# A sixteen-stage kernel: query blocks of the causal attention in another order, zero products ahead of units, and the last block of latent keys projected later

## The chip, the core and the metric

The kernel runs on one core of a Trainium2 chip. The core has a matrix engine (TensorE, PE in the profile; its weight loads are shown as PEld), a vector engine (VectorE, DVE), an engine for activations (ScalarE, ACT), GpSimd (POOL) and SyncE (SP), whose queue issues the transfers. TensorE reads SBUF and writes PSUM. The metric is the time of one execution on the device in microseconds.

## The reference

The reference is a chain of sixteen residual layers on `x` of 2048 tokens by 128 features: `x = x + f(layernorm(x))`, for four blocks of two mixers and two feed-forward layers each. Two of the mixers matter here.

- `L0_attn_b` is causal attention with 16 heads of width 8, with a rotary embedding of queries and keys: `q`, `k` and `v` are projected with biases, `q` and `k` are turned by cosines and sines of the position, scores above the diagonal are masked, softmax over the keys, product with `v`, projection `Wp`. In the kernel this is the stage `Causal`.
- `L1_attn_b` is latent attention with 8 heads: queries and keys come from 32 latent features each plus 32 rotary-like features (`W_QR`, `W_KR`), the scores are taken over all 2048 keys with the scale 1/sqrt(160), softmax, product with values from the latent ones, projection `W_O`. In the kernel this is the stage `Mla`.

## The kernel before

The tokens stand in four blocks of 512 (`NB`, `BW`), 128 tokens to a tile. The stages run one after another: CumSum, Moe0, Causal, Moe0, Mamba, Mla, Ssm, Moe2, Attn2, Moe2, Hale, Moe3, Filtered, Moe3. `Core.run` (line 69) interleaves them in program order: while the `main` of one stage runs, `feed` (line 114) opens the next stage and runs its `early(b)` for the blocks whose `x` is final, as `Stage.blocks` (line 227) lets it: a block starts when the `final` of the stage before exceeds its number. All stages before Hale are handed to a scheduler that orders each engine's instructions by its own time line, so the order on an engine is not that of the program text. Within the attention stages, the products that pass through `in_turn` (line 657) keep their program order on TensorE.

**Causal** (`Attn16`, lines 685 to 949). `early(b)` normalizes a block (`normed`, `turned`), projects values, makes the rotated key heads (`heads`, line 732: eight products into two banks, cosine and sine tables loaded from memory, two VectorE products, one POOL add, a split into two rounded parts) and copies them into key slots `at_KT` (`slot`, line 754), four groups `g` of four heads with a row offset for each head. Blocks 0 to 2 are done beside the stage before. Block 3 (`own = 1`) is done beside the first units, by the generator `left`, one step for each step of pass A. `heads("q", 0)` is called at the start of `main`.

The work is cut into units `(g, b)`, 16 in all, in the order of `units` (line 604): for each query block `b` from 0 to 3 its four groups. Each unit is done twice. Pass A (line 807) computes the scores query by key and takes the largest on VectorE (`at_mx`, line 833; on diagonal tiles after adding a mask, line 832). The negative maximum is transposed and written by transfers (`at_mT`, `at_q`, lines 852 and 854) into two spare rows of the unit's queries. Pass B (line 861) computes the scores key by query (line 900), masks the diagonal tile by a product (line 903), takes the exponential on ScalarE (line 906), and multiplies with the values into the accumulator `ps_c` (line 879). Four products of a 128x32 zero tile `zerob` with a tile of ones follow each of these (line 883). Unit (g, b) has b+1 chunks of 512 keys in either pass. Pass A runs ahead of pass B by one unit and some steps. After the last group of a block, `out` (line 935) adds the projected result to `x` (line 948) and sets `final`.

**Mla** (`Mla`, line 1307 on). `early(b)` normalizes, makes queries `ml_QT`, latent features `ml_Z` and values, and then for each of the 8 heads a key block: a product with `G` (line 1406) and `combine` (line 1371), that is a ScalarE copy, a second product that adds the rounding error (line 1376) and a ScalarE copy into `ml_KT` (line 1377). All four blocks are complete before `main`. `main` closes the pools down to `sm`, allots its own and runs 17 units (the first one in two halves): pass A (line 1443, reduction line 1444), the maximum by `ml_mT` into `ml_pad` (lines 1464 and 1466), pass B (lines 1496, 1498, 1483).

## Time and profile before

| quantity | value |
|---|---|
| median of three runs | 4843.47 us |
| the runs | 4835.28, 4843.47, 4845.85 us |
| profiled execution | 4842.59 us |
| its span, first to last instruction | 4840.6 us |
| mean granted TensorE clock | 0.922 |
| Causal, first pass A product to last add to `x` | 318.2 to 860.9 us |
| Mla, products of pass B | 1320.3 to about 1927 us |

The page gives busy time of each engine, the span in 40 slices of 121 us with a digit for each (tenths busy; for `PEclk`, tenths of full TensorE clock), and the chain of work that ended last. A table by stretch gives start:end and length, then the busy time and number of instructions of each engine, the mean granted clock of TensorE, the share in which the transfer engines were busy and GB/s. A line of the timeline gives start, duration, engine, line, operation, output and inputs, shapes, count, and in brackets the idle time before it with what ended it.

### The profile page before, as it was taken

The numbers are of one execution on the slowest core, as the hardware profiler recorded it, in microseconds if no ns is written. First come the engines' busy times: TensorE is split into PE (matmuls) and PEld (weight loads), VectorE is DVE, ScalarE is ACT, GpSimd is POOL, SyncE is SP. The second block draws the span as 40 slices with busy tenths as digits, with TensorE's granted clock in tenths as the row PEclk, the third lists the DMA queues.
The fourth block names the chain that finished last, engine by engine and source line by source line (L and its number), as shares of the span: only waits on it lengthen the run. The fifth ranks groups of instructions, "written<-read, shape, count | busy, mean of one in ns | idle before, by whom it ended". The sixth has DMA issues, their size and how long they took to land.

```text
span 4840.6 us, 89173 instructions
## 1 busy us (share of the span) xinstructions
PE 4411.5 (91%) x36388; PEld 2496.4 (52%) x36388; DVE 3713.6 (77%) x5694; ACT 3052.4 (63%) x5570; POOL 947.6 (20%) x826
## 2 busy tenths in 40 slices
PE   6979999988799998799999999989988989999998
PEld 4744444655344443463444457656656634444466
DVE  7867886689666653789999958457768879999777
ACT  4634667775355555356888875345546648888876
POOL 4730000544100000330000013012215600000056
PEclk9966899998699999888999999889998969999999
DMA  1010000000000000000000000112211000000000
GB/s 52 6 45 6 4 2 9 22 1 17 17 14 14 18 14 4 8 1 2 2 2 2 2 4 12 33 50 51 51 48 37 9 8 2 2 2 2 2 20 7
DMA packets 69484, 73.33 MB, mean 15 GB/s; under 512 B 17616, under 2 KB 44102, under 8 KB 69076
## 3 DMA queue, kind: packets, MB, share of 16 engines
q1 hardware_dynamic: 69076, 67.64, 5.0%
q8 instruction: 287, 4.70, 0.4%
q14 instruction: 121, 0.99, 0.1%
HBM read 32.09 MB, written 1.05 MB: 7 GB/s over the span
## 4 chain that ended last, share of the span: by engine, by line
PE 68%; DVE 21%; ACT 5%; issue 3%; POOL 2%; DMA 1%; SPq 0%; POOLq 0%; ACTq 0%; DVEq 0%
PE ps_c L879 15%; PE ps_a L829 10%; PE ps_c L1483 5%; DVE at_mx L833 4%; PE ps_b L900 4%; PE ps_a L1443 3%; PE ps_c L883 3%; PE ps_b L1496 3%; PE ps_b L148 2%; PE ps_a L148 2%; PE ps_a L150 2%; PE ps_b L149 2%; PE ps_a L149 2%; PE ps_b L150 2%; DVE m_hl L455 1%
## 5 line engine op out<-in xcount | busy, mean ns | idle before, releaser
L906 ACT ACTIVATE at_P<-ps_b 128x512 f32<-128x512 f32 (+2 forms) x2688 | 1414.4, 581 | 335.0 <-PE ps_b L900 211.1
L833 DVE TENSOR_REDUCE at_mx<-ps_a 128x2 f32<-128x1024 f32 (+2 forms) x1344 | 1537.7, 1184 | 106.5 <-PE ps_b L900 66.8
L879 PE MATMUL ps_c<-at_P,at_V 128*32 128x256 f32 (+3 forms) x10752 | 868.3, 396 | 7.8 <-ACT at_u L888 7.3
L900 PE MATMUL ps_b<-at_q,at_KT 32*128 32x512 f32 (+2 forms) x2688 | 759.5, 499 | 6.6 <-DMA at_q<-at_mT 5.0
L829 PE MATMUL ps_a<-at_KT,at_q 32*128 32x512 f32 (+3 forms) x2688 | 701.1, 521 | 48.0 <-DVE at_mx L833 45.7
L829 PEld LDWEIGHTS ps_a<-at_KT,at_q 32*128 32x128 f32 x2688 | 267.1, 196 | 497.4 <-issue 338.1
L1444 DVE TENSOR_REDUCE ml_mx<-ps_a 128x2 f32<-128x1024 f32 x256 | 305.4, 1222 | 216.4 <-PE ps_a L1443 215.4
L454 ACT ACTIVATE m_hh<-ps_a,moe_b 128x512 fp32r<-128x512 f32 x512 | 349.8, 689 | 189.1 <-DVE m_h L451 158.0
L455 POOL TENSOR_TENSOR m_hl<-m_h,m_hh 128x512 fp32r<-128x512 f32 x256 | 360.5, 1409 | 541.1 <-ACT m_hh L454 529.3
L1498 ACT ACTIVATE ml_P<-ps_b 128x512 f32<-128x512 f32 (+1 forms) x544 | 272.5, 576 | 231.8 <-PE ps_b L1496 229.7
L879 PEld LDWEIGHTS ps_c<-at_P,at_V 128*32 128x32 f32 x10752 | 215.8, 110 | 359.2 <-issue 181.0
L883 PE MATMUL ps_c<-wide,zerob 128*32 128x256 bf16 x5184 | 391.1, 282 | 0.0
L266 POOL TENSOR_TENSOR ln_rs<-ln_ve,nhalf 128x4 f32<-128x4 f32 x56 | 61.8, 1104 | 1650.3 <-DVE ln_ve L264 1641.4
L900 PEld LDWEIGHTS ps_b<-at_q,at_KT 32*128 32x128 f32 x2688 | 326.3, 189 | 73.5 <-issue 44.2
L455 DVE TENSOR_TENSOR m_hl<-m_h,m_hh 128x512 fp32r<-128x512 f32 x256 | 257.1, 1005 | 79.4 <-ACT m_hh L454 77.9
L453 ACT ACTIVATE m_h<-ps_a,moe_b 128x512 f32<-128x512 f32 x320 | 220.6, 690 | 77.1 <-DVE m_hl L455 42.0
L1483 PE MATMUL ps_c<-ml_P,ml_V 128*33 128x512 f32 (+3 forms) x1088 | 257.5, 596 | 2.9 <-ACT ml_P L1498 2.9
L148 PE MATMUL ps_b<-m_hh,moe_w2h 128*128 128x512 f32 x512 | 221.7, 433 | 20.7 <-DVE m_t L475 17.8
L149 PE MATMUL ps_b<-m_hl,moe_w2h 128*128 128x512 f32 x512 | 213.9, 418 | 26.4 <-DVE m_hl L455 20.7
L148 PE MATMUL ps_a<-ln_h,moe_w1h 128*128 128x512 f32 x512 | 218.7, 428 | 10.7 <-ACT m_hh L454 10.6
L883 PEld LDWEIGHTS <-zerob 128*32 128x32 bf16 x5184 | 156.1, 100 | 113.6 <-issue 10.8
L149 PE MATMUL ps_a<-ln_l,moe_w1h 128*128 128x512 f32 x512 | 207.4, 405 | 0.0
(655 smaller groups left out, 7759.7 us busy)
## 6 DMA issues: line engine op xcount, KB each, us to landing
hl_KS<-hl_pkh SPq DMA_DIRECT2D x160, 64.0 KB
moe_w_raw<-in_l0f_W SPq DMA_DIRECT2D x32, 256.0 KB
ml_pad<-ml_QT SPq DMA_DIRECT2D x32, 256.0 KB
moe_w_raw<-in_l3f_W SPq DMA_DIRECT2D x32, 256.0 KB
hl_KS<-hl_pkl SPq DMA_DIRECT2D x80, 64.0 KB
at_pad<-at_q SPq DMA_DIRECT2D x64, 64.0 KB
at_q<-at_mT SPq DMA_DIRECT2D x192, 4.0 KB
at_cosT<-in_cosT SPq DMA_DIRECT2D x8, 256.0 KB
```

Source lines behind the costliest of these rows:

```text
L148: nc.tensor.matmul(out, lh, rh, start=start, stop=False)
L149: nc.tensor.matmul(out, lh, rl, start=False, stop=False)
L454: nc.scalar.activation(hh, ph, AF.Relu, bias=bias)
L455: (nc.gpsimd if f in ((0, 2) if self.spare else MS) else nc.vector).tensor_tensor(hl, h, hh.bitcast(F32), ALU.subtract)
L829: self.in_turn(nc.tensor.matmul(pa[:, k, :w], q[r, i * P : (i + 1) * P], KT[r, ch * BW : ch * BW + w], start=True, stop=True))
L833: nc.vector.tensor_reduce(mx[:, i, 2 * jj : 2 * jj + 2, ch], pa[:, :, :w], AX.X, ALU.max)
L879: self.in_turn(nc.tensor.matmul(self.acc[32 * j : 32 * j + 32, s], self.V[:, kt, h : h + 32], ps[j][:, s], start=start, stop=stop))
L883: self.in_turn(nc.tensor.matmul(self.acc[32 * j : 32 * j + 32, z], c.zerob, c.wide[:, z], start=False, stop=False))
L900: self.in_turn(nc.tensor.matmul(pbs[k][:, off:end], KT[r, kt * P : (kt + 1) * P], q[r, off:end], start=True, stop=not diag))
L906: nc.scalar.activation(p[:, off:end], pbs[k][:, off:end], AF.Exp, scale=scale)
L1444: nc.vector.tensor_reduce(mx[:, i, :, ch], pa, AX.X, ALU.max)
L1483: self.in_turn(nc.tensor.matmul(self.acc[64 * j : 64 * j + m, s], v, ps[k][j][:, s], start=kt + k == 0, stop=kt + k == NT - 1))
```

## The change

In Causal:

- The query blocks are taken in the order 0, 2, 3, 1 (`order`). `final` rises only over blocks that are all through (`over`).
- `heads("q", 0)` moves from `main` to the end of `early(0)`.
- Cosine and sine tables have two buffers each, and the split heads of keys and queries share two tiles with two buffers each (`twice`).
- Ahead of pass B of each unit of blocks 0 and 1 (`warmed`) stand six products of a 128x128 zero tile with 512 columns of ones. For the first unit they write a bank of their own, later they add zero to the accumulator.

In Mla:

- For block 3, `early` stops after the values; the eight key heads become the generator `left`. Pass A draws from it until the heads that it needs are there (`heads`), and one more at each step (`tick`).
- Ten zero products stand ahead of the transposes of block 3's normalized tokens.
- The pool `ml_e`, which the key heads use, now outlives the start of `main`; `ml_mT`, `ml_u` and `ml_Y` have one buffer in place of two.

```diff
-        self.zerob = self.per.tile([P, 32], BF16, name="zerob")
+        self.zerob = self.per.tile([P, P], BF16, name="zerob")
...
+    def zeros(self, n, to=None):
+        first = to is None
+        to = self.ps("c") if first else to
+        return [self.nc.tensor.matmul(to, self.zerob, self.wide, start=first, stop=first) for _ in range(n)]
...
-        units = [(g, b, 0, 4) for b in range(NB) for g in range(4)]
+        units = [(g, b, 0, 4) for b in self.order for g in range(4)]
...
+    def over(self, b):
+        self.through.add(b)
+        while self.final in self.through:
+            self.final += 1
...
         for _ in self.project(b, ln):
             yield
+        if b == self.order[0]:
+            self.qhl = self.heads("q", b)
+            yield
...
-            cos, sin = [c.load(self.pre_k, "at_" + n, (P, BW), c.ins[n][:, s], bufs=1) for n in ("cosT", "sinT")]
+            cos, sin = [c.load(self.pre_k, "at_" + n, (P, BW), c.ins[n][:, s], bufs=self.twice) for n in ("cosT", "sinT")]
...
-        h, l = (self.pre_k.tile([P, BW], F32R, name=f"at_{which}{k}", bufs=1) for k in "hl")
+        h, l = (self.pre_k.tile([P, BW], F32R, name=f"at_{which if self.twice == 1 else ''}{k}", bufs=self.twice) for k in "hl")
...
-        self.qhl = self.heads("q", 0)
         self.prep(0, 0)
...
-        if g == 3 and b + 1 < NB:
-            self.need(b + 2)
-            self.qhl = self.heads("q", b + 1)
+        if g == 3 and b != self.order[-1]:
+            b1 = self.order[self.order.index(b) + 1]
+            self.need(b1 + 1)
+            self.qhl = self.heads("q", b1)
...
         q, KT = self.qb[(g, b)], self.KT[g]
+        if b in self.warmed:
+            for i in c.zeros(6, self.acc):
+                self.in_turn(i)
...
-        self.final = b + 1
+        self.over(b)
...
 class Causal(Attn16):
...
+    order = (0, 2, 3, 1)
+    warmed, twice = (0, 1), 2
...
+    def tick(self):
+        if self.heads[-1]:
+            next(self.left, None)
...
         xn = self.normed(b)
         yield
+        if b == NB - 1:
+            c.zeros(10)
         ln = self.turned(xn)
...
+        if b < NB - 1:
+            yield from self.keys(b, Z)
+        else:
+            self.left = self.keys(b, Z)
+
+    def keys(self, b, Z):
+        c, nc = self.c, self.c.nc
         for h in range(8):
             pk = c.ps("b")
             nc.tensor.matmul(pk, self.G[:, h, :], Z, start=True, stop=True)
-            self.combine(self.KT[h][:, s], pk, self.lomask)
+            self.combine(self.KT[h][:, b * BW : (b + 1) * BW], pk, self.lomask)
+            self.heads[b] = h + 1
             yield
...
         for n, (i, ch) in enumerate(steps):
-            self.need(ch + 1)
+            while self.heads[ch] < 2 * g + 2:
+                next(self.left)
...
-            mT = self.wk.tile([4, BW], F32R, name="ml_mT")
+            mT = self.wk.tile([4, BW], F32R, name="ml_mT", bufs=1)
...
-                self.u = self.wk.tile([P, BW], F32, name="ml_u")
+                self.u = self.wk.tile([P, BW], F32, name="ml_u", bufs=1)
...
-            self.Y[b] = self.wk.tile([P, 4, 8, 32], F32, name="ml_Y")
+            self.Y[b] = self.wk.tile([P, 4, 8, 32], F32, name="ml_Y", bufs=1)
```

More of the change, by code (lines that the diff above doesn't have):

```diff
@@ L568 @@
     pace = 12
+    order = tuple(range(NB))
     lead = 0.15
@@ L576, in start @@
     def start(self):
-        self.have, self.count = NB - self.own, 0
+        self.have, self.count, self.through = NB - self.own, 0, set()
         self.left = self.blocks(self.have, NB)
@@ L677, in finish_late @@
         while self.closed != u:
-            if u == (3, NB - 1, 0, 4):
+            if u == (3, self.order[-1], 0, 4):
                 self.later(2)
@@ L690 @@
     finish = Attention.finish_late
-    causal, rope = False, False
+    causal, rope, twice = False, False, 1
+    warmed = ()
     scale = 1.0 / math.sqrt(8.0)
@@ L708, in open_kv @@
         self.V, self.Vh = paired_values(self.c.nc, wp, NT, "at_V")
-        self.Y, self.qb, self.hl, self.late, self.due, self.closed = {}, {}, {}, [], [], None
+        self.Y, self.qb, self.hl, self.late, self.due, self.closed, self.acc = {}, {}, {}, [], [], None, None
     def weights(self, wp):
@@ L882, in av @@
                 if not (kt == nkt - 1 and half):
-                    self.in_turn(nc.tensor.matmul(self.acc[32 * j : 32 * j + 32, z], c.zerob, c.wide[:, z], start=False, stop=False))
+                    self.in_turn(nc.tensor.matmul(self.acc[32 * j : 32 * j + 32, z], c.zerob[:, 0:32], c.wide[:, z], start=False, stop=False))
             if kt == nkt - 1 and half:
@@ L1366, in open_kv @@
         nc.gpsimd.memset(self.V0, 0.0)
+        self.pre_k = self.pool("ml_e", 2)
         self.open_ln()
-        self.pre_k = self.pool("ml_e", 2)
         self.npad, self.qb, self.Y, self.late, self.due, self.closed = 0, {}, {}, [], [], None
+        self.heads = [0] * NB
+    def tick(self):
+        if self.heads[-1]:
+            next(self.left, None)
     def combine(self, dst, src, mask):
@@ L1415, in main @@
         self.wk = self.pool("ml_k", 2)
-        self.start()
+        self.have, self.through = NB, set()
         self.prep(0, 0)
@@ L1533, in out @@
         nc.vector.tensor_tensor(xb, po, xb, ALU.add)
-        self.final = b + 1
+        self.over(b)
 class Ssm(Stage):
```

## The prediction

> **What bounds the kernel now.** I read the page first (shares, then the slices with the granted clock, then the chain), then tables of busy time over stretches that I cut at the units of the two stages the change touches, then the timeline of VectorE and TensorE where a stretch looked wrong.

> ```profile
> span 4840.6 us, 89173 instructions
> PE 4411.5 (91%) x36388; PEld 2496.4 (52%) x36388; DVE 3713.6 (77%) x5694; ACT 3052.4 (63%) x5570; POOL 947.6 (20%) x826
> ...
> PEclk9966899998699999888999999889998969999999
> ...
> PE 68%; DVE 21%; ACT 5%; issue 3%; POOL 2%; DMA 1%; SPq 0%; POOLq 0%; ACTq 0%; DVEq 0%
> ```

> TensorE carries 68% of the chain, but its clock falls to 0.6 in slices 3 and 4 (242 to 484 us, where Causal starts) and in slice 11 (1210 to 1331 us, where Mla starts). The table by stretch (busy us and count of PE, PEld, DVE, ACT, POOL; then the clock) says what that is worth:

> ```profile
> 284.00:318.00 34.00, 21.90 (x58) 12.36 (x58) 13.00 (x22) 11.06 (x18) 5.92 (x5) 0.54 0.26 79
> 318.00:388.00 70.00, 62.12 (x406) 29.12 (x409) 48.62 (x93) 23.75 (x54) 2.53 (x2) 0.50 0.05 17
> 388.00:504.00 116.00, 109.63 (x1040) 51.20 (x1032) 87.05 (x153) 58.07 (x129) 3.57 (x3) 0.70 0.02 6
> 504.00:639.00 135.00, 127.94 (x1528) 59.08 (x1528) 121.67 (x166) 90.85 (x190) 3.39 (x13) 0.92 0.02 4
> 639.00:813.00 174.00, 169.47 (x2025) 76.02 (x2025) 152.02 (x186) 123.27 (x250) 1.02 (x1) 0.90 0.01 2
> 813.00:861.00 48.00, 45.63 (x577) 21.74 (x565) 1.66 (x5) 38.15 (x80) 0.81 (x1) 1.00 0.06 19
> ...
> 1276.00:1287.00 11.00, 6.48 (x20) 4.15 (x20) 6.71 (x24) 2.14 (x7) 3.54 (x3) 0.69 0.10 39
> 1287.00:1306.00 19.00, 18.23 (x26) 7.99 (x26) 0.29 (x1) 8.99 (x17) 0.00 (x0) 0.50 0.16 62
> 1306.00:1321.00 15.00, 11.95 (x26) 5.31 (x24) 13.20 (x14) 1.04 (x3) 0.00 (x0) 0.61 0.00 0
> ```

> The first six rows are Causal: head, pass A of query blocks 0, 1, 2, 3, and the last pass B. A chunk is 512 keys of one unit; blocks 0 to 3 hold 4, 8, 12, 16 chunks. At clock 0.92 block 2 takes 135/12 = 11.2 us a chunk with VectorE at 90%; block 1 at 0.70 takes 116/8 = 14.5 with VectorE at 75%; block 0 at 0.50 takes 17.5. So a warm TensorE leaves VectorE as the bound, a slow one binds itself. The last three rows are the start of Mla: 19 us in which TensorE projects keys at half clock and VectorE does nothing. VectorE's timeline names it: its next reduction waits 19.69 us for the scores.

> ```profile
> 1284.94 2.35 DVE L1444 TENSOR_REDUCE ml_mx<-ps_a 128x2 f32<-128x1024 f32 x2
> 1306.98 5.75 DVE L1444 TENSOR_REDUCE ml_mx<-ps_a 128x2 f32<-128x1024 f32 x5 [19.69 <-PE ps_a L1443]
> ```

> **Part 1, first query heads in `early`, two buffers for cos, sin and heads.** Before, after the last key slot of block 2, TensorE starts the query heads at 306.17 and the first pass A product runs at 318.24. In the changed order of instructions these 8 products stand behind block 1's key heads, and the query slots follow block 2's key slots at once. The moved chain is 306.17 to 313.68 (8 products, 2 VectorE products, 1 POOL add, 1 ACT cast, 1 VectorE subtraction). Its place is idle: TensorE sits 6.29 us before 289.67. Its two loads (cos, sin) move on SP's queue ahead of the Moe weight loads; those have until 861. Gain 8 us. Bounds: 12.07 (318.24-306.17) if all goes, 3.7 if block 2's heads, which share the single `at_r0`, are pushed by one rotation (L747 at 298.21 to `at_kl`'s end at 303.98, 5.8 us; 9.5-5.8). I take -8, near the first, since 290.4 to 298.2 is free on that chain.

> **Part 2, six zero products before each unit of blocks 0 and 1.** 48 products of 128x512. Nearest rows: products of 512 columns follow each other every 0.43 us at clock 0.5 (306.89 to 307.49 and on) and every 0.23 us at 1.0 (860.27, 860.50, 860.73). Block 0: 24 x 0.43 = 10.3 us, on the path, because TensorE is busy 62 of 70 us there. Against it: if the runs lift the clock, block 0 is bounded by VectorE's 48.6 us, a gain of at most 70-48.6 = 21. Ends +10.3 and -21. The clock did rise for single windows at denser moments in 388 to 504, and the runs are back to back over all 128 columns, so I take a net -5. Block 1: 24 x 0.23 = 5.5 us, hidden under VectorE if warm (I put 0), 10.3 if cold. The runs carry no wait of their own; behind each stand the next score products, and VectorE's reductions wait for those.

> [...]

> **Part 3, order 0, 2, 3, 1.** Counting each slot as the larger of pass A of a unit and pass B of the one before, both orders need 44 chunks: the long last pass B (4 chunks) becomes 2 for block 1's last unit, and 2 are lost where block 3's last pass B stands beside block 1's first pass A. So the order alone is worth nothing; what counts is that block 1's units no longer come straight after the cold start. Ends of pass A by the casts to `at_mT`: 388.0 | 415.8, 445.8, 472.8, 503.8 | 534.4, 573.7, 606.3, 638.6 | 676.9, 727.5, 766.9, 813.2; end 861. Changed: block 2's units 31+36+32.5+32.5 (36 between 39.3, which follows block 1, and 32.6), block 3's 38.3+50.6+39.4+46.3, block 1's first 44 (the pass B beside it ran 813 to 855 alone), its others 3x25 (11.2 a chunk gives 22.4; block 1's rows gave 27 to 31 at clock 0.70), last pass B and `out` 27 (21+6). Sum 452.6 against 473: -20. Bounds: 3x22.4 and 32.6 give -32; 3x30 and 39.3 give -2.

> **Part 4, Mla: keys of block 3 beside pass A, ten zeros.** From 1287 to the first pass B product at 1320.3 are 33 us. In the changed order 11 score tiles and 8 key heads interleave, all before that product. VectorE: 11 x 1.15 (5.75/5) = 12.7. TensorE warm: a head took about 1.25 us at 1267 to 1275 and a tile of two scores 0.47, so 8x1.25+11x0.47 = 15.2; cold: 2.13 a head (1294.0 to 1305) and 0.73 a tile, 25. With the 2.5 us for the maximum's transpose and load: 17.7 or 27.5, a gain of 15 or 5.5. The ten zeros cost 10x0.23 = 2.3 us; the first waits for VectorE's add out of the one `ps_c` bank (1275.41 to 1276.1), and behind them stands the transpose that waits for `ln_xn` until 1279.39 (idle 3.77). So they cost 0; without that gap 2.3. They fill the idle time ahead of the drop to 0.50, so I take -13, nearer the warm end. Bounds -17 (chain 1279 to 1287 faster too) and -3. One buffer for `ml_mT`, `ml_u`, `ml_Y`: the next write comes a unit later (16 units in some 620 us, 39 us each), the readers take about 1 us: 0.

> **Sum.** -8-5-20-13 = -46 on the profiled execution's own 4842.6 us (span 4840.6 and 2.0 around it): 4796.6. The median of the runs shown is 0.9 higher, so I predict **4797 us**. The three runs spread 10.6 us; 0.2% (9.7 us) is what a measurement can tell.

> **Rivals.** (a) The zeros do not move the clock: +10.3 in block 0, order at -2, heads -8, Mla -13: -13, 4830. For it: 70 us of near-full TensorE at 0.50. Against it: the zero run is 128 columns wide, what ran there mostly 32. Chance 0.2. (b) Everything warms: -12-21-32-17 = -82, 4761; VectorE's floors speak for it, the restless clock at every change of block (0.70 to 0.92) against it. Chance 0.1. (c) Slower: block 2 is entered cold. It then runs at 14.5 instead of 11.2 us a chunk, 3.3 x 12 = +40; with block 1 at 30 a unit (+15), zeros +15 against the forecast, Mla at the cold end (+8): -46+78 = +32, 4875. It decides once 14 chunks (46/3.3) run slow. For it: three times the work now follows the cold start directly. Against: its 8 unmasked key tiles of 12 per unit; block 0 is all masked ones. Chance 0.1. (d) Forecast, 0.6, own range 4770 to 4822.

> Faster: 0.6+0.1+0.15 of (a) = 0.85; within 0.2%: 0.04 of (a); slower: 0.1+0.01 = 0.11. The range 4766 to 4834 takes in (a) and the ends of the forecast, leaving out (c) and most of (b).

> **What would show it.** Right: first pass A product near 310; clock above 0.6 in block 0's units and about 0.9 in block 1's at the end; Causal's last `x` add near 827; in Mla no VectorE wait over 5 us for scores after 1240 and clock above 0.8 there. Wrong: clock 0.5 until well into block 2, block 1's units at 30 us, or key heads at 2.1 us beside the scores.

## The result and the profile after

The change made the kernel a little slower. Twenty runs of it have a median of 4853.75 us (4839.13 to 4867.13); twenty of the kernel before, 4841.91 us. The ratio is 1.0023, with a 95% interval of 1.0014 to 1.0032. The prediction, 4797 us, is 57 us too low and outside its own range. The profiled execution took 4860.15 us.

The first lines of the page of the changed kernel, and its slices of the granted clock:

```profile
span 4858.0 us, 89266 instructions
PE 4425.0 (91%) x36417; PEld 2506.6 (52%) x36446; DVE 3706.1 (76%) x5694; ACT 3052.9 (63%) x5570; POOL 951.5 (20%) x826
...
PEclk9976888998799999798999999889998979999999
```

TensorE is busy 13.5 us longer than before (4425.0 against 4411.5). In the clock's row, slices 3 and 11, where the first zero products stand, did rise (6 to 7 in both), but slices 6 and 7 (607 to 850 us), blocks 3 and 1, fell from 9 to 8. The table by stretch, cut at the ends of pass A as the prediction's rows were (start:end and length, busy us and count of PE, PEld, DVE, ACT, POOL, then the clock):

```profile
310.00:381.00 71.00, 63.40 (x432) 30.64 (x436) 51.82 (x97) 24.33 (x55) 2.53 (x2) 0.62 0.05 16
381.00:423.00 42.00, 33.85 (x254) 15.29 (x258) 28.62 (x35) 9.88 (x29) 0.00 (x0) 0.58 0.01 1
423.00:539.00 116.00, 111.03 (x1188) 50.92 (x1184) 92.98 (x147) 74.30 (x149) 4.58 (x14) 0.81 0.01 2
539.00:727.00 188.00, 180.19 (x2044) 78.82 (x2032) 155.42 (x183) 125.84 (x255) 1.28 (x1) 0.85 0.01 3
727.00:761.00 34.00, 33.67 (x398) 14.93 (x392) 19.79 (x28) 25.55 (x52) 0.00 (x0) 0.90 0.01 2
761.00:857.00 96.00, 89.93 (x972) 41.55 (x971) 60.13 (x88) 55.23 (x119) 0.00 (x0) 0.84 0.01 2
857.00:888.00 31.00, 28.47 (x354) 14.36 (x347) 1.21 (x4) 19.09 (x45) 0.00 (x0) 0.97 0.08 27
```

The rows are block 0 (71 us, 70 before); block 2's first unit (42) and its others (116); block 3 (188, before 174); block 1's first unit (34) and its others (96); the last pass B. Blocks 2, 3 and 1 with the last pass B take 42 + 116 + 188 + 34 + 96 + 31 = 507 us, where the same work took 473 before and the prediction had 452.6. Causal's last add to `x` runs at 887.6 us instead of 860.2. From there to the end the changed kernel is the faster one (3970 against 3980 us).

Mla did what was forecast. TensorE's timeline there:

```profile
1303.78 2.32 PE L129 MATMUL ps_c<-wide,zerob 128*128 128x512 bf16 x9 [0.85 <-DVE x L1117]
1307.02 0.33 PE L283 MATMUL ps_b<-ident,ln_xn 128*128 128x128 f32 x1 [0.92 <-DVE ln_xn L276]
```

The zero run fills the gap before the transpose that waits for `ln_xn`. Key heads and scores now alternate. The first pass B product is at 1335.45 us, 15.1 later than before (1320.32), while the transpose above came 27.6 later (1279.39 before): a gain of 12.5.

What went wrong in Causal is seen at the end of a unit. VectorE first, then TensorE, in block 3 of the changed kernel:

```profile
623.95 2.36 DVE L851 TENSOR_REDUCE at_mx<-ps_a 128x2 f32<-128x1024 f32 x2
626.22 0.21 DVE L860 TENSOR_REDUCE at_m<-at_mx 128x16 f32<-128x64 f32 x1
626.46 0.18 DVE L862 CAST at_mhl<-at_m 128x16 fp32r<-128x16 f32 x1
626.54 1.22 DVE L851 TENSOR_REDUCE at_mx<-ps_a 128x2 f32<-128x1024 f32 x1
627.68 0.16 DVE L863 TENSOR_TENSOR at_mhl<-at_m,at_mhl 128x16 fp32r<-128x16 f32 x1
```

```profile
625.83 0.29 PE L924 MATMUL ps_b<-at_maskbT,identb 128*128 128x128 bf16 x2
627.99 0.40 PE L868 MATMUL ps_b<-identr,at_mhl 128*8 128x128 f32 x4 [1.87 <-DVE at_mhl L863]
```

When pass A of a unit is done, VectorE makes the negative maximum (L860), casts it (L862) and subtracts (L863), and TensorE transposes the result (L868). Here a reduction of the next unit (L851, 1.22 us) stands on VectorE between the cast and the subtraction. These products keep their program order on TensorE (`in_turn`), so it stands still for 1.87 us. Three neighbouring stretches of 3.41 us of the same kernel (columns as above) show what follows:

```profile
623.05:626.47 3.42, 3.07 (x42) 1.29 (x38) 3.35 (x6) 2.48 (x6) 0.00 (x0) 1.00 0.00 0
626.47:629.88 3.41, 1.89 (x30) 1.01 (x34) 1.71 (x4) 1.25 (x4) 0.00 (x0) 1.00 0.00 0
629.88:633.29 3.41, 3.41 (x35) 1.21 (x28) 2.11 (x2) 1.14 (x4) 0.00 (x0) 0.50 0.11 29
```

TensorE is busy 1.89 of 3.41 us in the stretch with the wait, and in the next one the granted clock is 0.50. It stays there for 13.7 us. In blocks 2, 3 and 1 of the changed kernel this wait comes at six of the twelve unit ends (1.05 to 2.01 us), in the kernel before at two (472 and 676 us; the first of them below). None of the code around it was edited. The scheduler gives VectorE its order, and the edits moved the scheduler's time line.

```profile
472.35 0.40 PE L850 MATMUL ps_b<-identr,at_mhl 128*8 128x128 f32 x4 [2.02 <-DVE at_mhl L845]
```

The first two sets of runs test other theories; the third tests this wait.

### The profile page after: what moved, and what is told of

Read it like the earlier page. It is cut to its first block, busy times and chain, and to the rows that moved or that the text cites. A ratio compares the mean times of both kernels' runs of the same rounds, so it can differ in the third digit from the quotient of the medians.

```text
span 4858.0 us, 89266 instructions
## 1 busy us (share of the span) xinstructions
PE 4425.0 (91%) x36417; PEld 2506.6 (52%) x36446; DVE 3706.1 (76%) x5694; ACT 3052.9 (63%) x5570; POOL 951.5 (20%) x826
## 3 DMA queue, kind: packets, MB, share of 16 engines
HBM read 32.09 MB, written 1.05 MB: 7 GB/s over the span
## 4 chain that ended last, share of the span: by engine, by line
PE 57%; DVE 16%; ACT 4%; issue 3%; POOL 1%; DMA 1%; SPq 0%; POOLq 0%; ACTq 0%; DVEq 0%
PE ps_c L900 12%; PE ps_a L847 8%; PE ps_c L1524 5%; PE ps_a L1484 3%; PE ps_b L1537 3%; PE ps_b L921 3%; PE ps_c L904 2%; DVE at_mx L851 2%; PE ps_a L155 2%; PE ps_a L157 1%; PE ps_a L156 1%; PE ps_b L155 1%; PE ps_b L156 1%; PE ps_b L2185 1%; PE ps_b L157 1%
## 5 line engine op out<-in xcount | busy, mean ns | idle before, releaser
L851 DVE TENSOR_REDUCE at_mx<-ps_a 128x2 f32<-128x1024 f32 (+2 forms) x1344 | 1539.7, 1183 | 141.7 <-PE ps_b L921 71.5
L927 ACT ACTIVATE at_P<-ps_b 128x512 f32<-128x512 f32 (+1 forms) x2688 | 1414.7, 581 | 361.3 <-PE ps_b L921 223.8
L900 PE MATMUL ps_c<-at_P,at_V 128*32 128x256 f32 (+2 forms) x10752 | 869.5, 397 | 7.5 <-ACT at_u L909 6.9
L921 PE MATMUL ps_b<-at_q,at_KT 32*128 32x512 f32 (+1 forms) x2688 | 763.0, 501 | 4.9 <-DMA at_q<-at_mT 4.3
L904 PEld LDWEIGHTS <-zerob 128*32 128x32 bf16 x5184 | 156.2, 101 | 113.8 <-issue 10.6
L157 PE MATMUL ps_a<-ln_h,moe_w1l 128*128 128x512 f32 x512 | 208.6, 408 | 0.3 <-DVE moe_w1l L150 0.3
```

The source lines that it names most:

```text
L157: nc.tensor.matmul(out, ll, rh, start=False, stop=stop)
L851: nc.vector.tensor_reduce(mx[:, i, 2 * jj : 2 * jj + 2, ch], pa[:, :, :w], AX.X, ALU.max)
L900: self.in_turn(nc.tensor.matmul(self.acc[32 * j : 32 * j + 32, s], self.V[:, kt, h : h + 32], ps[j][:, s], start=start, stop=stop))
L904: self.in_turn(nc.tensor.matmul(self.acc[32 * j : 32 * j + 32, z], c.zerob[:, 0:32], c.wide[:, z], start=False, stop=False))
L921: self.in_turn(nc.tensor.matmul(pbs[k][:, off:end], KT[r, kt * P : (kt + 1) * P], q[r, off:end], start=True, stop=not diag))
L927: nc.scalar.activation(p[:, off:end], pbs[k][:, off:end], AF.Exp, scale=scale)
```

## First set: the parts, alone and left out

The theories at that point: "lumps" (score tiles and pass B steps interleave badly on TensorE), "zeros" (the zero runs cost more than forecast) and "clock" (the first large block is entered at half clock). The sets ran on different chips; the kernel before, run beside each, took 4840.0 to 4843.3 us. A profile is one execution, up to 26 us off its kernel's median, so times are compared by medians and profiles are read for orders and waits. The diffs are shortened.

**Only the Mla part.** Causal's classes stay as before; the edits in `Mla` (key heads of block 3 by `keys`, ten zeros, buffers) stay.

```diff
 class Causal(Attn16):
-    order = (0, 2, 3, 1)
-    warmed, twice = (0, 1), 2
...     # in early
-        if b == self.order[0]:
-            self.qhl = self.heads("q", b)
...     # in main
+        self.qhl = self.heads("q", 0)
```

> Only the Mla part of the change (part 4 of the prediction), Causal as before. All theories agree here: the first pass B product of Mla comes 12 to 13 us earlier relative to the end of Mamba, as in the profile of the changed kernel (27.6 us late at the last block's transposes, 15.1 us late at the first pass B product). Total 10 to 14 us under the kernel before, ratio 0.997 to 0.998. If the gain is lost later in the Ssm stage, ratio 1.000.

Measured: 4823.12 us, ratio to before 0.9970 (0.9959 to 0.9982). By the ratio the Mla part is worth 14.5 us (9 to 20), and the forecast of 13 holds.

**Only the order.** The kernel before with `order`, `over` and the changed `prep`.

```diff
 class Causal(Attn16):
+    order = (0, 2, 3, 1)
```

> Only the order 0, 2, 3, 1 in Causal, no zeros, heads and Mla as before. Theory 'lumps' (TensorE takes the products of passes A and B in program order; where a unit of pass A has three chunks beside one of pass B it waits for VectorE to free the score banks, and then runs pass B alone while VectorE idles, whatever the clock): Causal ends 25 to 35 us later than before (about 888), VectorE idles about 13 us in block 2's first slot. Theory 'zeros' (the runs of zero products are what costs): Causal within 8 us of 861. Theory 'clock' (block 2 entered cold and kept cold): later by 25 to 40 us, but with a clock of 0.6 or less over block 2's units.

Measured: 4859.70 us, ratio 1.0035 (1.0018 to 1.0053). The order alone loses 19 us, where the prediction had it gain 20. In its profile Causal's last add comes at 888.2 us, as "lumps" had it.

**All but the order.**

```diff
-    order = (0, 2, 3, 1)
     warmed, twice = (0, 1), 2
```

> The changed kernel with the natural order 0, 1, 2, 3 (zeros ahead of units of blocks 0 and 1, query heads early, Mla part). Lumps: the loss is gone, Causal ends 5 to 10 us before 861 (heads -8, zeros about 0 to +8), total 10 to 22 us under before, ratio 0.9955 to 0.998. Zeros: Causal still 10 to 20 us late, total near before. Clock: as lumps, with a clock over 0.75 in block 1's units, because the zeros now stand where the cold stretch is (0.56 and 0.59 there before).

Measured: 4857.30 us, spread from 4824.29 to 4878.28, ratio 1.0027 (1.0004 to 1.0050). So the loss is not the order's alone, and "lumps", which had it gone here, misses.

**All but the zeros ahead of units.**

```diff
-    warmed, twice = (0, 1), 2
+    warmed, twice = (), 2
```

> The changed kernel without the runs of six zeros ahead of units in Causal (order 0, 2, 3, 1, heads early, Mla part). Lumps: no better than the changed kernel, Causal ends within 8 us of 888, ratio 1.000 to 1.003. Zeros: Causal ends near 855, total 15 to 25 us under before. Clock: worse than the changed kernel, Causal past 895, since nothing lifts the clock in block 0.

Measured: 4822.86 us, ratio 0.9966 (0.9954 to 0.9978): 31 us less than the change. Forty-eight products take at most 48 x 0.43 = 20.6 us if every one ran at half clock and on the path (at clock 0.50 the kernel before starts products of 512 columns 0.43 us apart, at 307.49 and 307.92 us). The zeros cost more than the time they take, and the loss did not lie only where they stand: block 3 has none, and from its first unit's end to the end of its pass A it took 150 us with them (577 to 727) and 135 without (577 to 712).

## Second set: where the zeros cost, and by what

**Heads and Mla, old order, no zeros.**

```diff
-    order = (0, 2, 3, 1)
-    warmed, twice = (0, 1), 2
+    warmed, twice = (), 2
```

> The early query heads with two buffers and the Mla part, in the old order and without the zero products of the units. The prediction's order part (-20) says that this loses 20 us against the same with the new order (4822.9): 4843. The theory "lumps" (three or four score tiles of a heavier unit beside each short pass B step, in order on TensorE, so that a slot is longer than the larger of the two passes) says that the old order is no worse: the Mla part alone gave 4823.1, the heads take 8 us off, 4815.

Measured: 4826.63 us, spread from 4801.41 to 4871.92, ratio 0.9979 (0.9951 to 1.0007). The median lies beside the kernel with the new order (4822.86), but the difference is 4 us with an interval of -7 to 26, too wide to rule out the 20.

**Zeros in block 0 only, and in block 1 only.**

```diff
-    warmed, twice = (0, 1), 2
+    warmed, twice = (0,), 2      # and, in the other kernel, (1,)
```

> The change with zero products only ahead of block 0's four units. Theory "duration" (the products cost their own time and nothing else): 4822.9 + 24 x 0.43 = 4833. Theory "clock" (runs of zeros move the later drops of the granted clock to worse places or make them longer, also in blocks that have no zeros): more than that, 4838 to 4854. The prediction (net -5, the clock rises in block 0): 4818.

> The change with zero products only ahead of block 1's four units, the last of the stage. The prediction (hidden under VectorE): 4823. Theory "duration": TensorE is the bound in block 1, 24 x 0.23 to 0.43 = 5.5 to 10.3, so 4828 to 4833. Theory "clock": beyond 4836.

Measured: 4843.52 us (ratio 1.0006, 0.9995 to 1.0016) and 4841.86 us (1.0002, 0.9992 to 1.0011), so each half costs 19 to 21 us, twice the 10.3 us of 24 products at half clock. With zeros only in block 0, Causal's profile is as long as without them up to block 3 (first unit's end at 577 in both), and then 15 us longer in block 3.

**The zeros narrowed to 32 columns of the array.**

```diff
-            for i in c.zeros(6, self.acc):
-                self.in_turn(i)
+            to = c.ps("c") if self.acc is None else self.acc
+            for _ in range(6):
+                self.in_turn(nc.tensor.matmul(to[0:32], c.zerob[:, 0:32], c.wide, ...))
```

> The change with the zero runs ahead of the units narrowed from 128 to 32 columns of the zero tile, the same number and the same 512 moving columns, so that each takes the same time at the same clock but works a quarter of the array. Theory "duration": as the change, 4854. Theory "clock" by the width (full-array products draw the drops): 4822.9 plus the products' own 11 to 20 us, 4834 to 4843.

Measured: 4856.59 us, ratio 1.0035 (1.0021 to 1.0048), the same as the change (4853.75). How many columns of the zero tile they use made no difference here.

So neither their width nor their duration explained the loss. The wait shown above does better. In the kernel without zeros the same unit end looks like this (VectorE, then TensorE):

```profile
623.71 0.22 DVE L860 TENSOR_REDUCE at_m<-at_mx 128x16 f32<-128x64 f32 x1
623.96 0.18 DVE L862 CAST at_mhl<-at_m 128x16 fp32r<-128x16 f32 x1
624.17 0.18 DVE L863 TENSOR_TENSOR at_mhl<-at_m,at_mhl 128x16 fp32r<-128x16 f32 x1
624.26 2.35 DVE L851 TENSOR_REDUCE at_mx<-ps_a 128x2 f32<-128x1024 f32 x2
```

```profile
624.36 0.29 PE L924 MATMUL ps_b<-at_maskbT,identb 128*128 128x128 bf16 x2
624.50 0.40 PE L868 MATMUL ps_b<-identr,at_mhl 128*8 128x128 f32 x4
```

The three small instructions stand together and TensorE does not wait. Unit ends with a wait over 0.95 us, among the twelve of the last three blocks, by kernel: two before, two with only the Mla part, two with only the order, two without the zeros, three in the one with heads and Mla, four each with zeros in one block and without the order, six with all zeros, wide or narrow. Of the kernels with the Mla part, those with four or six are the slow ones (4842 us and up, the others 4827 and less). The kernel before, without that part, took 4842 with two waits. Only the order alone doesn't fit: 4860 us with two waits, 20.5 us of half clock after each.

## Third set: VectorE's order held

The theory is now "chain": the loss is the wait for the subtraction and the lost clock behind it. It is tested by holding VectorE's instructions of pass A in Causal to the program's order, with the same token that holds TensorE's products. No instruction is added or left out.

```diff
+    def in_step(self, i):
+        if self.pre == "l0b_":
+            self.c.tc.stamp_issue_order_token(i.ins, self.pre + "dve")
...
-                nc.vector.tensor_reduce(mx[...], pa[:, :, :w], AX.X, ALU.max)
+                self.in_step(nc.vector.tensor_reduce(mx[...], pa[:, :, :w], AX.X, ALU.max))
...     # likewise the mask add, the reduction to at_m, the cast and the subtraction
```

**The change, held.**

> The change, with the order of pass A's VectorE instructions in Causal held to that of the program: at the end of a unit the reduction to at_m, the cast and the subtraction then stand together, where in the change a reduction of the next unit (1.2 us) stands ahead of the subtraction in 6 of the 12 units of blocks 2, 3 and 1. Theory "chain" (TensorE, in order, waits 1.1 to 2.0 us for the subtraction at each of these unit ends, and the granted clock halves in the window after): six times (1.7 us and some 7 us of lost clock) go, 4853.8 - 6 x 8.7 = 4802, and no TensorE wait for at_mhl over 0.5 us is left in these blocks. Theory "zeros" (the runs of zeros cost their own time at half clock, 31 us): 4845 to 4854.

Measured: 4818.38 us, ratio to before 0.9949 (0.9936 to 0.9962). A second set of runs of the same kernel:

> The change with held VectorE order once more, for its interval and a second profile. Theory "chain": 4818, within 7 us. If the first six times were a lucky draw: 4835 to 4854.

Measured: 4829.85 us, ratio 0.9983 (0.9974 to 0.9992). The two differ by 11 us, so the second time lies between the two expectations. Over all 17 runs the median is 4827.7, 26 us under the change (95% interval 21 to 36, by resampling the runs): holding VectorE's order takes back most of the 31 us that the zeros cost, though not the 52 of the expectation (4802). Causal's last add comes at 861.1 us in the first profile and at 854.7 in the second, instead of 887.6. A unit end of block 3 in the second:

```profile
659.89 0.22 DVE L864 TENSOR_REDUCE at_m<-at_mx 128x16 f32<-128x64 f32 x1
660.14 0.18 DVE L866 CAST at_mhl<-at_m 128x16 fp32r<-128x16 f32 x1
660.35 0.18 DVE L867 TENSOR_TENSOR at_mhl<-at_m,at_mhl 128x16 fp32r<-128x16 f32 x1
```

What kept the transposes waiting, by the view of the tile `at_mhl` over the whole run (us and times), in the change and then in the held kernel:

```profile
  DVE at_mhl L863: 11.5, 8
```

```profile
  DVE at_mhl L867: 1.1, 1
```

The one left is in a later stage.

**The same without the zeros, new and old order of blocks.**

```diff
+    # in_step as above
-    warmed, twice = (0, 1), 2
+    warmed, twice = (), 2        # and, in the other kernel, no order line
```

> New order, early heads and Mla part, without the zero products of the units, VectorE's unit ends held together. Theory "chain": two such unit ends go against 4822.9, so 4822.9 - 2 x 8.7 = 4806; beside the change with held unit ends it shows what the zeros cost by themselves, 24 x 0.43 + 24 x 0.23 = 16 us at most where nothing hides them. Theory "zeros": 4823, 31 us under the change with held unit ends.

> The same in the old order of blocks. Theory "chain": three such unit ends go against 4826.6: 4800; the order is worth the difference to the kernel with the new order, which the prediction put at 20 us (so 4826 here if that is right) and the theory "lumps" at nothing or less.

Measured: 4823.48 us, ratio 0.9967 (0.9955 to 0.9979), in the new order and 4816.58 us, 0.9955 (0.9935 to 0.9975), in the old. Both are 17 us above what "chain" expected (4806 and 4800). In the old order that is 10 us under the unheld kernel (4826.63; interval of the difference -6 to 34). In the new order holding changed nothing (4822.86 unheld): the two waits were gone, yet from 290 to 850 us its profile has the same 205 us at half clock as the unheld one, 157 of them in one piece from 290 us on. What zeros cost by themselves: 4827.7 with them, 4823.5 without, so 4 us (interval -5 to 13) and not 31.

**The subtraction put late.** Held order, new order of blocks, no zeros, but the subtraction goes behind the next unit's first reduction.

```diff
-        self.in_step(nc.vector.tensor_tensor(mhl[:, I, :, 1], ..., ALU.subtract))
+        self.sub = lambda: self.in_step(nc.vector.tensor_tensor(mhl[:, I, :, 1], ..., ALU.subtract))
...
                 self.in_step(nc.vector.tensor_reduce(mx[...], pa[:, :, :w], AX.X, ALU.max))
+                self.subtract()
...     # and, where it is still to come, at the head of turn(), before the transposes
+            self.subtract()
```

> New order, without the zero products of the units, VectorE's order held, but the subtraction put behind the first reduction of the next unit at every unit: 11 of the 12 units of blocks 2, 3 and 1 then have a reduction in the chain, with nothing added and no product more. Theory "chain": 4806 + 11 x 5 to 9 = 4861 to 4905. Rival "clock by itself" (the drops come whatever VectorE's order): within 11 x 1.2 = 13 us of the kernel without it, 4806 to 4836.

Measured: 4836.20 us, ratio 0.9993 (0.9982 to 1.0005). It costs 12.7 us (interval 3 to 23) at eleven units: the rival's number, not the theory's. Its profile says why. At the unit end where the change waited 1.87 us, it has

```profile
623.28 0.29 PE L939 MATMUL ps_b<-at_maskbT,identb 128*128 128x128 bf16 x2
624.44 0.40 PE L883 MATMUL ps_b<-identr,at_mhl 128*8 128x128 f32 x4 [0.87 <-ACT at_P L942]
```

TensorE comes later to its transposes here: the mask product before them ends 0.9 us after the unit's last reduction (623.57 and 622.63), in the change 0.2 us ahead of it (626.12 and 626.31). Eight waits are 0.66 to 1.05 us long, and after none of these did the clock fall at once. After one of 1.49 us it did, for 30.7 us. So a reduction in the chain is not enough; the clock fell behind the one long wait. This run therefore doesn't test what six long waits cost.

How long is long can be counted over the nineteen profiles of this case. Unit ends in the last three blocks that were reached at full clock, by TensorE's wait before the transposes; "at once" is a fall from the start of the wait to 3.4 us behind its end:

| wait | unit ends | followed by half clock at once | half clock after, mean over all |
|---|---|---|---|
| under 0.5 us | 155 | 3 | 0.5 us |
| 0.5 to 0.95 us | 6 | 0 | 0 |
| 0.95 to 1.3 us | 12 | 9 | 11 us |
| 1.3 to 2.1 us | 26 | 25 | 16.8 us |

In the change the six waits add up to 10.3 us, with 102.5 us at half clock behind them. All unit ends of the held kernels, but for the late subtraction, stand in the first row: where holding took a long wait out, the fall at once nearly always went with it.

## Fourth set: the order of the blocks, and the best version

**Zeros, heads and Mla in the old order, held.**

```diff
+    # in_step as above
-    order = (0, 2, 3, 1)
     warmed, twice = (0, 1), 2
```

> Old order of blocks, with the zero products ahead of the units, early heads and Mla part, VectorE's unit ends held together. Without holding this gave 4857.3, with a reduction in the chain at four units of blocks 1 to 3; without the zeros, held, 4816.6. Theory "chain" (the zeros lose by what they do to VectorE's order): 4817, between 4811 and 4827. Theory "zeros" (they lose by themselves): 4833 to 4857.

Measured: 4811.56 us, ratio 0.9951 (0.9938 to 0.9965). Unheld this was 4857.30, so holding gives 46 us here (interval 21 to 60). A second set of runs:

> The old order with zeros, early heads, Mla part and held unit ends once more. The change with held unit ends came out at 4818.4 and then 4829.9, so a repeat may lie 11 us off: 4811 to 4823 if the first result stands; near 4827, if it is no better than the same with the new order.

Measured: 4811.81 us, ratio 0.9928 (0.9905 to 0.9951). Over both, twelve runs have a median of 4811.6, 29 us under the kernel before (interval 21 to 34): the lowest median of the case. Against the same kernel without zeros (4816.6) the zeros gain 5 us (interval -9 to 17). In block 0 the best case looks like this: its units from the end of the first pass A on, with the zeros and then without, both held and in the old order.

```profile
331.00:371.00 40.00, 37.19 (x375) 17.71 (x377) 31.39 (x59) 19.26 (x47) 1.27 (x1) 0.91 0.05 16
```

```profile
334.00:384.00 50.00, 47.88 (x352) 21.88 (x356) 31.94 (x59) 19.45 (x47) 1.27 (x1) 0.50 0.04 13
```

Here the clock is 0.91 against 0.50 and the units take 40 us against 50; in the profile of the second set the same three units took 47 us. Over all of block 0, from the first pass A product, the eight profiles with zeros there have a mean clock of 0.62 to 0.77 and take 62.6 to 72.5 us, on average 69. Of the eleven without, nine stay at 0.50 and two come to 0.60 without any zeros; they take 67.1 to 74.8 us, on average 72. So a higher clock goes with the zeros in block 0, but the time differs by some 2.5 us, not 10.

**Only the order, held, and only the holding.**

```diff
 class Causal(Attn16):          # the kernel before, with in_step
+    order = (0, 2, 3, 1)       # in one of the two
```

> Only the order 0, 2, 3, 1, VectorE's unit ends held together. Unheld it gave 4859.7, with a reduction in the chain at two units. The prediction's part 3 as it was meant: 20 us under the kernel before with held unit ends. Theory "lumps" (slots are longer than the larger pass): 10 to 20 us over it. Theory "even": within 7 us of it, since 44 chunks stand in both orders and the loss of the order alone came from where the clock fell.

> The kernel before with VectorE's unit ends in Causal held together, nothing else. A reduction stood in the chain at two units with a wait of TensorE over 1 us (472 and 676 us). Theory "chain": up to two drops of the clock go, 4840.4 - 2 x 8.7 = 4823; if drops come at other places as in the held kernel with the new order, 4835 to 4841.

Measured: 4840.13 us (ratio 1.0003, 0.9990 to 1.0017) with the order and 4841.65 us (1.0001, 0.9992 to 1.0010) without. Held, the order alone is worth nothing either way (-1.5 us, interval -6 to 11); unheld it lost 19 us, and holding took back 20 (interval 5 to 28). And holding alone gives the kernel before nothing. In its profile Causal ends 9 us earlier (851.1 against 860.2), 6 of them are gone by 2408 us, and the span is the same. There the six middle units of the later attention stage show waits of 0.70 us that the kernel before hasn't, because that stage was scheduled anew as well. It is so in all six pairs: from Causal's last add to the end, the profile of the held kernel is 4 to 18 us longer than that of the unheld one, though `in_step` holds Causal alone. In the kernel without zeros, which gained nothing, Causal ends 4.2 us earlier when held (849.6 against 853.8), and what follows takes 5.4 us longer. Two profiles of one kernel differ there by 3 to 7 us, so a single pair shows little; that all six go one way shows more.

What holding gave doesn't go by the number of waits that it took out: 26 us for six, 46 and 20 for four and two (all but the order, only the order), 10 for three (heads and Mla, interval -6 to 34), nothing for two (all but the zeros, and the kernel before).

## Why the prediction was wrong, step by step

- **Part 1, heads, -8: right.** The first pass A product runs at 310.00 us; it was 318.24. (The 9.5 us in its lower bound come from no row.)
- **Part 2, zeros, net -5: the products' own price right within the noise, wrong in what it left out.** Held, the zeros measure +4 in the new and -5 in the old order, both with zero in the interval, and the clock in block 0 is higher with them (a mean of 0.62 to 0.77 against 0.50 to 0.60), though not each time as far as was argued. (That it had risen "for single windows" in 388 to 504 us misread the clock: it was full there for 3.4, 17 and 14 us and from 492 on.) The failed sentence is "The runs carry no wait of their own; behind each stand the next score products". It prices the time of the products and not what they do to VectorE's order. Inserted instructions also move the scheduler's time line, and with it the order of VectorE behind them: six unit ends with a reduction in the chain where the kernel without zeros has two, 26 us by holding, 31 by leaving the zeros out. The prediction compared orders of instructions for the steps that were edited, not for the chain at each unit's end, where this stood.
- **Part 3, order, -20: wrong in two ways.** The slots came out at 507 us in place of 452.6; of these 54 us, 30 went when the unit ends were held (378 to 855 us in the second profile, 477 us). The other 24 are the model "the larger of pass A of a unit and pass B of the one before": block 2's first two slots took 42 and 41 us, held, where 31 and 36 were forecast (in the first, TensorE was busy 34 of the 42 and at clock 0.58), its last two 34 and 32 (32.5 each), block 1's first 41 (44), its others 34, 21 and 26 (25 each). Block 3's were 37, 55, 43 and 40, 175 in sum as forecast. So a heavier unit beside a short pass B took longer than the larger of the two. It was also entered at half clock, as rival (c) had it; no run separates the two. Held, the order alone comes to nothing (-1.5 us); beside the other parts it costs 16 us with the zeros (4827.7 against 4811.6, interval 6 to 22) and 7 without (-9 to 21).
- **Part 4, Mla, -13: right**, 12.5 in the profile and 14.5 alone.
- **Rivals.** (a) and (b) took the zeros' own effect as the question, which was not it. (c) had the right sign and a part of the cause: block 2 took 158 us, 26 more than forecast, where (c) had 40 more, and still 18 more when held. No rival had an engine's order change where nothing was edited.
- **What would show it** said clock above 0.6 in block 0 and about 0.9 in block 1 (0.62 and 0.84 to 0.90 measured), and the last add near 827 (887.6). The first was met. Of the signs of being wrong, half clock in block 2 came for its first slot (0.58), and block 1's units took 34, 40, 25 and 32 us ("at 30"). Against the forecast block 2 lost 26 us, block 3 13, block 1 11 and the last pass B 3; the list names no sign in block 3, and holding took its 13 away whole.

In the table of unit ends above, a wait of TensorE of 1.3 to 2.1 us was followed at once by half clock in 25 of 26 cases, one under 0.5 us in 3 of 155.

What stays open: why some waits cost much more than others, whether block 2's first slots are long by the interleaving or by the clock, and how much of the differences under 10 us comes from the later stages, which every edit schedules anew.

## What to carry to other kernels

Where a scheduler orders the engines, an inserted instruction costs what it does to the order of the others too: list the changed order of every engine over the chains that another engine waits for, not only around the edit. Pin such a short chain to the program's order before judging any other edit; the same edits that lost 12 us here (or 17 in the old order) then won 12 to 29. Judge the pin by the whole time too, since it schedules the later stages anew. And read a wait of TensorE with the clock of the 15 us behind it: in the change six waits of 10.3 us in sum stood where Causal took some 30 us more.

## What the hardware showed beyond that

```
window at full clock, busy under 0.6:  67 of  75 followed by half clock
                      busy 0.6 to 0.9: 74 of 349
                      busy over 0.9:   23 of 1704
window at half clock, busy under 0.85:   1 of 211 followed by full clock
                      busy 0.85 to 0.95: 16 of 109
                      busy over 0.95:   163 of 706
```

In these counts the two directions differ. A window at full clock in which TensorE stood still for 1.4 us or more was followed by half clock in 67 of 75 cases; a window at half clock that was busy over 0.95 was followed by full clock in only 163 of 706, and the half clock lasted 16.8 us on average behind the waits of 1.3 us and more. What else decides over the return was not found. The zero products, whole or narrow, are no certain way back: 133 us in one piece passed at half clock in the old order held without them (292 to 425 us), 44 us (68 in the second set's profile) and some short pieces with them.
